# A graph network whose destination one-hots come from TensorE instead of a DRAM broadcast

## The chip, the cores and the metric

The kernel runs on one core of a Trainium2 chip. The metric is the device time of one execution in microseconds (us): the median of 3 runs of the kernel before.

## The reference

There are 6250 nodes with 128 features, and 106,250 directed edges, sorted by destination, self loops among them. Two layers, each with a residual:

```
h = relu(layernorm(x))
m    = leaky_relu(h[src] @ Wl + bl + h[dst] @ Wr + br + ew1 * We)     # layer 1: GATv2
a    = softmax of (m @ att) over the edges of a destination
x    = x + batchnorm(gelu(h + sum over edges(a * (h[src] @ Wl + bl)) + bias))
h = relu(layernorm(x))
em   = relu(layernorm([h[src], h[dst]] @ msg_w + msg_b) * g + beta) * ew   # layer 2
mean = sum over edges(em) / number of edges of the destination
x    = x + gate * relu(layernorm([h, mean] @ upd_w + upd_b)...) + (1 - gate) * h
```

What an edge takes from its source is a row of a node table that lies in DRAM and is gathered by index. What it takes from its destination is spread from a window of the other table by a matmul with a one-hot matrix, as the edges are sorted by destination.

## The kernel before

**Sizes.** Nodes are 49 tiles of 128 (NT). Edges are padded to 832 × 128 and handled in 104 supersteps (NS) of 8 × 128 = 1024 edges (ST, SE). Within a superstep the destinations lie in a window of at most 126 nodes (WIN) above its first.

**Tables.** In lines 233 to 259 the node tiles go in groups of 7 (TG): bn_stats on VectorE, normalization and relu on ScalarE (L248), a transpose on TensorE (L251), a copy of hT by VectorE and ScalarE in turn (L253), a matmul to 257 columns (L255), the add of the bias (L256) for the source table xl and a ScalarE copy (L257) for the destination table xr. SyncE stores both to DRAM (xl_d L258, xr_d L259). After the first group the source indices are cast and transposed (L262). Then a flag read from the data picks general() or fast(); here it is fast().

**Preparation in fast()** (L744 to 843). The destinations relative to the window's first node, dl_b (bf16, one row per superstep), are stored to DRAM as dl_d, and also transposed into columns dl_c. Edge weights and segment marks become columns as well.

**First edge stage** (L886 to 1085). Its instructions keep the order in which they are written (manual_schedule). Superstep s: load(s + 2) has SyncE fetch the window W of the table (L854), row s of dl_d broadcast to 128 partitions (dlb, 256 KB, L856) and the edge weights as a row; GpSimd gathers the sources in 8 indirect DMAs (L196, 10 buffers gl); TensorE spreads the destinations of s + 1 (L867, 16 matmul records); VectorE adds (L1033); ScalarE does relu; a step of the segment maxima; the one-hot oh by destination of u = s − 7 is made (L1040), ScalarE scales the gathered rows (glw, L1049); VectorE multiplies by att and reduces (L1051, L1053); one_hot_t(s + 2) (L863) compares dlb with the partition's number, which gives the one-hot that spreads; TensorE aggregates u (L1063). Generators (nodes, turn) do the node work of finished windows in steps between supersteps.

**Middle** (to L1175): batch normalization, and the tables a_d and b_d of the second layer.

**Second edge stage** (L1177 to 1333), u = s − 1, also in written order: load, 8 gathers into 6 buffers gl1, spread1(s + 1) on TensorE (L867), VectorE's add y (L1298), ScalarE's 8 squares with their sums (L1303) and root (L1304), the store of an aggregate, the one-hot oh of u (L1309), 8 passes with mg_r (L1314), the add of mb_r (L1316), ScalarE's relu (L1317) and glw (L1320), one_hot_t(s + 2) (L863), the reciprocal (L1324), and the aggregation of u (L1329, 16 matmul records). nodes1 gives node work in steps at the end of a superstep (TensorE L1228 to 1269 through the PSUM tiles nt and nz, VectorE L1211 to 1273).

The lines that set the order in stage 2, before:

```
spread1(s + 1)                                   # PE
V.tensor_tensor(y, pss.pop(s), gl, ALU.add)      # DVE L1298
V.tensor_tensor(oh, ...)                         # DVE L1309
for j in range(ST): V.scalar_tensor_tensor(yu, ..., mg_r, ...)   # L1314
V.tensor_tensor(yu, yu, over_tiles(mb_r, ST), ALU.add)           # L1316
S.activation(yu, yu, AF.Relu)                    # ACT L1317
...
one_hot_t(*wins[s + 2])                          # DVE L863
...
T.matmul(aggs[u], oh[:, j, :], glw[:, j, :], ...)  # PE L1329
```

Of the kernel before, what the change touches and what calls it, by code (L numbers as in the profile page):

```python
# [9 lines left out]
F32 = mybir.dt.float32  # L10
# [6 lines left out]
P = 128  # L17
# [18 lines left out]
BT = K // NBT  # L36
WIN = 126
PACE = 60
SLACK = 96
# [9 lines left out]
def kernel(  # L49
# [36 lines left out]
    def flat(v, ap, offset=0):  # L86
        return bass.AP(tensor=v.tensor, offset=v.offset + offset, ap=ap)
# [5 lines left out]
    V.memset(x_sb[:, NT - 1, :], 0.0)  # L93
    for g in range(NG):
        n = TG if g < NG - 1 else TG - 1
        nc.sync.dma_start(
            x_sb[:, g * TG : g * TG + n, :],
            x[g * TG * P : (g * TG + n) * P, :].rearrange("(t p) f -> p t f", p=P),
        )
# [74 lines left out]
    def over_tiles(row, n):  # L174
        return row[:, None, :].to_broadcast([P, n, D])
# [24 lines left out]
    def node_rows(table, g, n=TG):  # L200
        return table[g * TG * P : (g * TG + n) * P].rearrange("(t p) ... -> p t ...", p=P)
# [16 lines left out]
    with tc.tile_pool(name="pre", bufs=2) as pp, tc.tile_pool(name="pre1", bufs=1) as p1, tc.tile_pool(  # L218
# [5 lines left out]
        wt = p1.tile([P, D], F32, name="wt")  # L224
        w0c = p1.tile([P, 2 * D + 1], F32, name="w0c")
        b0c = p1.tile([P, WL], F32, name="b0c")
        V.tensor_copy(w0c[:, WL:], w0[:, D:])
        for o, i in ((w0c, w0), (b0c, b0)):
# [3 lines left out]
            V.tensor_scalar(o[:, D : D + 1], o[:, D : D + 1], 0.2, None, op0=ALU.mult)  # L232
        for g in range(NG):
            mv = pp.tile([P, TG, 2], F32, name="mv")
            for j in range(TG):
                st = pp.tile([P, 6], F32, name="st")
                V.bn_stats(st, x_sb[:, g * TG + j, :])
                V.bn_aggr(mv[:, j, :], st)
            rstd = pp.tile([P, 2, TG], F32, name="rstd0")
            S.activation(rstd[:, 0, :], mv[:, :, 1], AF.Sqrt, bias=eps)  # L240
            V.reciprocal(rstd[:, 0, :], rstd[:, 0, :])
            V.scalar_tensor_tensor(rstd[:, 1, :], mv[:, :, 0], -1.0, rstd[:, 0, :],
                                   op0=ALU.mult, op1=ALU.mult)
            tl = pp.tile([P, TG, WL], F32, name="tl")
            tr = pp.tile([P, TG, D], F32, name="tr")
            for j in range(TG):
                h = pp.tile([P, D], F32, name="h")
                S.activation(h, x_sb[:, g * TG + j, :], AF.Relu, bias=rstd[:, 1, j : j + 1],  # L248
                             scale=rstd[:, 0, j : j + 1])
                tp = ps_p.tile([P, P], F32, name="tp")  # L250
                T.transpose(tp, h, ident)  # L251
                hT = h_sb[:, g * TG + j, :]
                (S.copy if j % 2 else V.tensor_copy)(hT, tp)  # L253
                mm = ps_p.tile([P, 2 * D + 1], F32, name="mm")
                T.matmul(mm, hT, w0c, start=True, stop=True)  # L255
                V.tensor_tensor(tl[:, j, :], mm[:, :WL], b0c, ALU.add)  # L256
                S.copy(tr[:, j, :], mm[:, WL:])  # L257
            nc.sync.dma_start(node_rows(xl_d, g), tl)  # L258
            nc.sync.dma_start(node_rows(xr_d, g), tr)  # L259
            if g == 0:  # L260
                sr = p1.tile([NS, SE], F32, name="sr")
                V.tensor_copy(sr, src_r)  # L262
                columns(ps_k, src_c, sr, "ctp")
# [477 lines left out]
    def fast():  # L741
# [6 lines left out]
        b_d = dram.tile([NP + P, D], F32, name="b_d")  # L748
        dl_d = dram.tile([NS, SE], BF16, name="dl_d")
        res0_d = [dram.tile([NP + P, W0], F32, name=f"res0_{i}") for i in range(2)]  # L750
# [3 lines left out]

        dl_c = fs.tile([P, NS, ST], F32, name="dl_c")
        ew_c = fs.tile([P, NS, ST], F32, name="ew_c")
# [3 lines left out]
        nc.sync.dma_start(base_row, flat(dst, [[1, 1], [SE, NS]]))  # L760

        def base_of(s):
            return nc.values_load(base_row[0:1, s : s + 1], engines=[mybir.EngineType.SP],
                                  min_val=0, max_val=NP - 1)

# [19 lines left out]
        with tc.tile_pool(name="col1", bufs=1) as p1, tc.tile_pool(name="rows", bufs=2) as rp, tc.tile_pool(  # L785
            name="ps_p", bufs=2, space=PSUM
        ) as ps_p:
# [4 lines left out]
            dl_b = p1.tile([NS, SE], BF16, name="dl_b")  # L792
            V.tensor_copy(dl_b, fr)
            nc.sync.dma_start(dl_d, dl_b)

# [49 lines left out]
        def zero(tables, n, i):  # L845

            for r in tables:
                nc.sync.dma_start(r.rearrange("(p k) f -> p (k f)", p=P)[:, i * 5 * n : (i + 1) * 5 * n],
                                  zt[:, : 5 * n])

        def load(pool, table, s, weights):

            w, oht = Ws[s % 3], ohts[s % 3]
            nc.sync.dma_start(w[:WIN], table[ds(base_of(s), WIN), :])  # L854
            dlb = pool.tile([P, SE], BF16, name="dlb")
            nc.sync.dma_start(dlb, flat(dl_d, [[0, P], [1, SE]], s * SE))  # L856
            if weights:
                nc.sync.dma_start(oht[WIN : WIN + 1, :], flat(edge_weight1, [[SE, 1], [1, SE]], s * SE))
            return w, dlb, oht

        def one_hot_t(w, dlb, oht):

            V.tensor_scalar(oht[:WIN, :], dlb[:WIN, :], iota_p[:WIN, :], None, op0=ALU.is_equal)  # L863

# [4 lines left out]
        def store(agg, tables, s):  # L869
            nc.sync.dma_start(tables[s % 2][ds(base_of(s), WIN), :], agg[:WIN, :])  # L870

        def fetch(fin, tables, t0, n):
# [13 lines left out]
        with tc.tile_pool(name="e0", bufs=2) as ep, tc.tile_pool(  # L886
# [3 lines left out]
        ) as ps_m, tc.tile_pool(name="ps_1", bufs=1, space=PSUM) as ps_1, tc.manual_schedule():  # L890
            iota_ps = ps_1.tile([P, P], F32, name="iota_ps")
            S.copy(iota_ps, iota_f)
            LAG = SB + 3
# [107 lines left out]
            def spread(s):  # L1001
                w, _, oht = wins.pop(s)
                pss[s] = ps_m.tile([P, ST, D], F32, name="m_ps")
                expand(pss[s], oht, w)
# [12 lines left out]
            for s in range(2):  # L1017
                one_hot_t(*wins[s])
            spread(0)
            for s in range(NS + LAG + 1):  # L1020
# [16 lines left out]
                if 0 <= u < NS:  # L1037
                    b, q = divmod(u, SB)
                    oh = ep.tile([P, ST, P], F32, name="oh")
                    V.tensor_tensor(oh, over_tiles(iota_ps, ST), over_features(dl_c[:, u, :], ST),  # L1040
                                    ALU.is_equal)
                    glw = ep.tile([P, ST, W0], F32, name="glw")
                    V.tensor_copy(glw[:, :, D:], exm[b][:, q])  # L1043
                if u >= 1:
                    flush(u - 1)
# [132 lines left out]
        with tc.tile_pool(name="e1g", bufs=6) as gp, tc.tile_pool(name="e1", bufs=2) as ep, tc.tile_pool(  # L1178
# [3 lines left out]
        ) as ps_m, tc.tile_pool(name="ps_11", bufs=1, space=PSUM) as ps_1, tc.manual_schedule():  # L1182
            iota_ps = ps_1.tile([P, P], F32, name="iota_ps1")
            S.copy(iota_ps, iota_f)
            glws = [e1.tile([P, ST, WL], F32, name=f"glw1_{i}") for i in range(3)]
# [6 lines left out]
            def spread1(s):  # L1192
                w, _, oht = wins.pop(s)
                pss[s] = ps_m.tile([P, ST, D], F32, name="y_ps")
                expand(pss[s], oht, w)
# [87 lines left out]
            for s in range(2):  # L1283
                one_hot_t(*wins[s])
            spread1(0)
            for s in range(NS + 2):
# [20 lines left out]
                if 0 <= u < NS:  # L1307
                    oh = ep.tile([P, ST, P], F32, name="oh1")
                    V.tensor_tensor(oh, over_tiles(iota_ps, ST), over_features(dl_c[:, u, :], ST),  # L1309
                                    ALU.is_equal)  # L1310
                    yu = ys.pop(u)
                    ru = rss.pop(u)
                    for j in range(ST):
                        V.scalar_tensor_tensor(yu[:, j, :], yu[:, j, :], ru[:, j : j + 1], mg_r,  # L1314
                                               op0=ALU.mult, op1=ALU.mult)
                    V.tensor_tensor(yu, yu, over_tiles(mb_r, ST), ALU.add)  # L1316
                    S.activation(yu, yu, AF.Relu)  # L1317
                    glw = glws[u % 3]
                    for j in range(ST):
                        S.activation(glw[:, j, :D], yu[:, j, :], AF.Copy, scale=ew_c[:, u, j : j + 1])  # L1320
                if s + 2 < NS:
                    one_hot_t(*wins[s + 2])
                if s < NS:
# [61 lines left out]
```

## Time and profile before

| what | value |
|---|---|
| median of 3 runs | 2407.45 us (2405.77 to 2409.37) |
| the profiled execution | 2414.23 us, its span 2412.4 us |
| granted TensorE clock, mean | 0.764 |
| busy: PE, DVE, ACT, POOL | 57%, 68%, 53%, 70% of the span |
| first edge stage, gathers | 71.6 to 1145.7 us |
| middle | 1145.7 to 1256.8 us |
| second edge stage, gathers | 1256.8 to 2355.2 us |
| DMA moved | 242.90 MB, mean 101 GB/s |

PE is TensorE, DVE VectorE, ACT ScalarE, POOL GpSimd, SP SyncE. A group row gives line, engine, operation, output<-input, count, then busy us, mean ns, and the engine's idle time before it with what ended it. A source row gives the minimum, median and maximum in ns, then the first and the last start in us. A row of waits gives the total in us, the times and the longest. A timeline row begins with start and duration in us. L12 is line 12 of the kernel.

### The profile page before, as it was taken

The numbers are of one execution on the slowest core, as the hardware profiler recorded it, in microseconds if no ns is written. First come the engines' busy times: TensorE is split into PE (matmuls) and PEld (weight loads), VectorE is DVE, ScalarE is ACT, GpSimd is POOL, SyncE is SP. The second block draws the span as 40 slices with busy tenths as digits, with TensorE's granted clock in tenths as the row PEclk, the third lists the DMA queues.
The fourth block names the chain that finished last, engine by engine and source line by source line (L and its number), as shares of the span: only waits on it lengthen the run. The fifth ranks groups of instructions, "written<-read, shape, count | busy, mean of one in ns | idle before, by whom it ended". The sixth has DMA issues, their size and how long they took to land.

```text
span 2412.4 us, 30614 instructions
## 1 busy us (share of the span) xinstructions
PE 1375.8 (57%) x7692; PEld 1270.8 (53%) x7692; DVE 1637.3 (68%) x3597; ACT 1276.6 (53%) x4267; POOL 1699.7 (70%) x1703
## 2 busy tenths in 40 slices
PE   6446555556566556565484555555655655555553
PEld 3345555555555455565464555555555654555553
DVE  6666677677677667767445567677767768768765
ACT  5223343334344334344456676676676677667663
POOL 1677777777777777777057777777777777777770
PEclk9667887787878777777687677778777777777876
DMA  6743455443443433443142333343333333333331
GB/s 166 211 114 92 111 151 137 98 100 92 101 100 92 98 96 92 100 100 80 32 132 79 90 94 99 85 107 97 83 107 97 85 108 103 83 101 102 85 96 30
DMA packets 217496, 242.90 MB, mean 101 GB/s; under 512 B 41373, under 2 KB 158077, under 8 KB 217309
## 3 DMA queue, kind: packets, MB, share of 16 engines
q0 software_dynamic: 53792, 110.57, 19.7%
q1 hardware_dynamic: 160657, 130.00, 18.5%
q8 instruction: 64, 1.05, 0.2%
q14 instruction: 123, 1.01, 0.1%
q10 hardware_dynamic: 2860, 0.27, 0.1%
HBM read 197.43 MB, written 43.25 MB: 100 GB/s over the span
## 4 chain that ended last, share of the span: by engine, by line
POOL 44%; issue 18%; DMA 14%; DVE 13%; PE 7%; ACT 3%; SPq 0%; DVEq 0%; another core or an unknown queue 0%; ACTq 0%; POOLq 0%
POOL gl L196 44%; DMA gl<-xl_d,src_c 7%; DMA gl<-a_d,src_c 5%; DVE y L1314 2%; DVE m_ps L1033 2%; PE agg_ps L1063 2%; DVE y L1298 1%; DVE oh L1309 1%; PE agg_ps L1329 1%; DVE y L1316 1%; PE mm L255 1%; PE mm L1156 1%; ACT sq L1303 1%; DVE oh L1040 1%; DVE oht L863 1%
## 5 line engine op out<-in xcount | busy, mean ns | idle before, releaser
L196 POOL DMA_INDIRECT gl<-xl_d,src_c x832 | 820.9, 987 | 308.8 <-issue 229.8
L196 POOL DMA_INDIRECT gl<-a_d,src_c x832 | 845.2, 1016 | 260.7 <-issue 234.3
L1329 PE MATMUL agg_ps<-glw,oh 128*128 128x129 f32 x1664 | 363.9, 403 | 485.7 <-ACT glw L1320 439.7
L1329 PEld LDWEIGHTS agg_ps<-glw,oh 128*128 128x128 f32 x1664 | 336.3, 298 | 505.8 <-ACT glw L1320 505.8
L1063 PE MATMUL agg_ps<-glw,oh 128*128 128x130 f32 x1664 | 345.0, 389 | 386.3 <-DVE glw L1043 206.8
L1063 PEld LDWEIGHTS agg_ps<-glw,oh 128*128 128x128 f32 x1664 | 320.7, 288 | 404.1 <-ACT glw L1049 404.1
L1034 ACT ACTIVATE m_ps<-m_ps 128x1024 f32<-128x1024 f32 x104 | 104.8, 1008 | 573.6 <-DVE m_ps L1033 429.3
L1303 ACT ACTIVATE sq<-y 128x128 f32<-128x128 f32 x832 | 257.1, 309 | 275.8 <-DVE y L1298 252.4
L1033 DVE TENSOR_TENSOR m_ps<-m_ps,gl 128x1024 f32<-128x1024 f32 x104 | 128.1, 1232 | 299.9 <-DMA gl<-xl_d,src_c 273.7
L867 PE MATMUL m_ps<-W,oht 128*128 128x128 f32 x1664 | 259.8, 320 | 36.2 <-DVE oht L863 22.8
L867 PEld LDWEIGHTS m_ps<-W,oht 128*128 128x128 f32 x1664 | 243.8, 233 | 45.2 <-issue 22.3
L1320 ACT ACTIVATE glw<-y,ew_c 128x128 f32<-128x128 f32 x832 | 254.4, 389 | 3.4
L1049 ACT ACTIVATE glw<-gl,exm 128x128 f32<-128x128 f32 x832 | 254.3, 394 | 0.0
L1298 DVE TENSOR_TENSOR y<-y_ps,gl 128x1024 f32<-128x1024 f32 x104 | 126.8, 1220 | 187.8 <-DMA gl<-a_d,src_c 146.7
L867 PE MATMUL y_ps<-W,oht 128*128 128x128 f32 x1664 | 230.4, 298 | 13.2 <-DVE oht L863 9.0
L867 PEld LDWEIGHTS y_ps<-W,oht 128*128 128x128 f32 x1664 | 226.7, 218 | 13.8 <-issue 13.8
L1314 DVE SCALAR_TENSOR_TENSOR y<-y,rs,mg_r 128x128 f32<-128x128 f32 x832 | 227.3, 344 | 0.0
L863 DVE TENSOR_SCALAR oht<-dlb,iota_p 126x1024 f32<-126x1024 bf16 x208 | 159.3, 766 | 15.1 <-DMA dlb<-dl_d 15.0
L1303 ACT ACTIVATION_READ_ACCUMULATOR sq<-y 128x1 f32 x832 | 155.0, 186 | 0.0
L1051 DVE TENSOR_TENSOR m_ps<-m_ps,att 128x1024 f32<-128x1024 f32 x104 | 131.3, 1263 | 4.8 <-ACT m_ps L1034 4.6
L1317 ACT ACTIVATE y<-y 128x1024 f32<-128x1024 f32 x104 | 109.9, 1057 | 41.1 <-DVE y L1316 41.0
L1316 DVE TENSOR_TENSOR y<-y,mb_r 128x1024 f32<-128x1024 f32 x104 | 127.7, 1228 | 3.6
(251 smaller groups left out, 1610.7 us busy)
## 6 DMA issues: line engine op xcount, KB each, us to landing
dlb<-dl_d SPq DMA_DIRECT2D x208, 256.0 KB
gl<-xl_d,src_c POOLq DMA_INDIRECT x832
gl<-a_d,src_c POOLq DMA_INDIRECT x832
res<-agg SPq DMA_DIRECT2D x104, 64.0 KB
res<-agg SPq DMA_DIRECT2D x104, 63.5 KB
W<-xr_d SPq DMA_DIRECT2D x104, 63.0 KB
W<-b_d SPq DMA_DIRECT2D x104, 63.0 KB
res<-zt SPq DMA_DIRECT2D x20, 325.0 KB
```

The lines of the kernel that those rows point to most:

```text
L196: GP.indirect_dma_start(out=dest, out_offset=None, in_=table, in_offset=bass.IndirectOffsetOnAxis(ap=idx, axis=0))
L863: V.tensor_scalar(oht[:WIN, :], dlb[:WIN, :], iota_p[:WIN, :], None, op0=ALU.is_equal)
L867: T.matmul(ps[:, j, :], oht[:, j * P : (j + 1) * P], w, start=True, stop=True)
L1033: V.tensor_tensor(ps, ps, gl[:, :, :D], ALU.add)
L1049: S.activation(glw[:, j, :D], glu[:, j, :D], AF.Copy, scale=exm[b][:, q, j, 1:2])
L1063: T.matmul(aggs[u], oh[:, j, :], glw[:, j, :], start=(j == 0), stop=(j == ST - 1))
L1298: V.tensor_tensor(y, pss.pop(s), gl, ALU.add)
L1303: S.activation(sq, y[:, j, :], AF.Square, accum_out=rs[:, j : j + 1])
L1314: V.scalar_tensor_tensor(yu[:, j, :], yu[:, j, :], ru[:, j : j + 1], mg_r, op0=ALU.mult, op1=ALU.mult)
L1316: V.tensor_tensor(yu, yu, over_tiles(mb_r, ST), ALU.add)
L1320: S.activation(glw[:, j, :D], yu[:, j, :], AF.Copy, scale=ew_c[:, u, j : j + 1])
L1329: T.matmul(aggs[u], oh[:, j, :], glw[:, j, :], start=(j == 0), stop=(j == ST - 1))
```

## The change

- The tables before the branch are made in groups of 6 tiles (PG), three tiles to a PSUM tile (PB), with one copy and one add for three; they hold the source table xl alone. The source indices are cast after the fourth group.
- The destination table xr is made in fast(), 13 chunks of up to 4 tiles (TN).
- dl_b stays in SBUF, and the DRAM copy and the broadcast loads are gone. one_hot_t handles one half of a superstep: TensorE spreads row s of dl_b to all partitions by a matmul with a column of a bf16 identity, into PSUM, and VectorE compares from there. The PSUM tile is one that the node work uses too (tag "mx" in stage 1, "nt" in stage 2). The first half stands ahead of the stage's passes on u, the second where the whole stood.
- The window's first node is loaded into a register once per superstep and kept for the store.
- The column numbers, mg_r and mb_r are copied to PSUM at the start of a stage and read from there.

```diff
@@ tables before the branch @@
-        for g in range(NG):
+        for t0 in range(0, NT, PG):
+            n = min(PG, NT - t0)
...
+            for q in range(0, n, PB):
+                k = min(PB, n - q)
+                tp = ps_p.tile([P, PB, P], F32, name="tp")
+                for j in range(q, q + k):
...
+                    T.transpose(tp[:, j - q, :], h, ident)
+                S.copy(h_sb[:, t0 + q : t0 + q + k, :], tp[:, :k, :])
+                mm = ps_p.tile([P, PB, WL], F32, name="mm")
+                for j in range(k):
+                    T.matmul(mm[:, j, :], h_sb[:, t0 + q + j, :], w0c, start=True, stop=True)
+                V.tensor_tensor(tl[:, q : q + k, :], mm[:, :k, :],
+                                b0c[:, None, :].to_broadcast([P, k, WL]), ALU.add)
...
-                (S.copy if j % 2 else V.tensor_copy)(hT, tp)
-                mm = ps_p.tile([P, 2 * D + 1], F32, name="mm")
-                T.matmul(mm, hT, w0c, start=True, stop=True)
-                V.tensor_tensor(tl[:, j, :], mm[:, :WL], b0c, ALU.add)
-                S.copy(tr[:, j, :], mm[:, WL:])
-            nc.sync.dma_start(node_rows(xl_d, g), tl)
-            nc.sync.dma_start(node_rows(xr_d, g), tr)
-            if g == 0:
+            nc.sync.dma_start(xl_d[t0 * P : (t0 + n) * P].rearrange("(t p) f -> p t f", p=P), tl[:, :n, :])
+            if t0 == 3 * PG:
@@ fast(), preparation @@
+            if s not in bases:
+                bases[s] = nc.values_load(base_row[0:1, s : s + 1], engines=[mybir.EngineType.SP],
+                                          min_val=0, max_val=NP - 1)
+            return bases[s]
...
-            nc.sync.dma_start(dl_d, dl_b)
+            for t0 in range(0, NT, TN):
+                n = min(TN, NT - t0)
+                rp_ = ps_x.tile([P, TN, D], F32, name="xr_ps")
+                for j in range(n):
+                    T.matmul(rp_[:, j, :], h_sb[:, t0 + j, :], w0[:, D:], start=True, stop=True)
+                tr = xp.tile([P, TN, D], F32, name="tr")
+                S.copy(tr[:, :n, :], rp_[:, :n, :])
+                nc.sync.dma_start(xr_d[t0 * P : (t0 + n) * P].rearrange("(t p) f -> p t f", p=P), tr[:, :n, :])
@@ fast(), helpers @@
+        def constants(pool, *rows_):
+            n = 1 + len(rows_)
+            t = pool.tile([P, n * P], F32, name="cst")
+            for k, r in enumerate((iota_f,) + rows_):
+                S.copy(t[:, k * P : (k + 1) * P], r)
+            return [t[:, k * P : (k + 1) * P] for k in range(n)]
...
-            dlb = pool.tile([P, SE], BF16, name="dlb")
-            nc.sync.dma_start(dlb, flat(dl_d, [[0, P], [1, SE]], s * SE))
...
-        def one_hot_t(w, dlb, oht):
-            V.tensor_scalar(oht[:WIN, :], dlb[:WIN, :], iota_p[:WIN, :], None, op0=ALU.is_equal)
+        def one_hot_t(pool, tag, s, k, w, oht):
+            es = slice(k * CH, (k + 1) * CH)
+            dlp = pool.tile([P, CH], F32, name="dlp", tag=tag)
+            T.matmul(dlp, ident_b[:NS, s : s + 1].to_broadcast([NS, P]), dl_b[:, es], start=True, stop=True)
+            V.tensor_scalar(oht[:WIN, es], dlp[:WIN, :], iota_p[:WIN, :], None, op0=ALU.is_equal)
@@ first edge stage, after oh and the copy into glw @@
+                if s + 2 < NS:
+                    one_hot_t(ps_1, "mx", s + 2, 0, *wins[s + 2])
                 if u >= 1:
                     flush(u - 1)
...
                 if s + 2 < NS:
-                    one_hot_t(*wins[s + 2])
+                    one_hot_t(ps_1, "mx", s + 2, 1, *wins[s + 2])
@@ second edge stage, after oh @@
+                if s + 2 < NS:
+                    one_hot_t(ps_1, "nt", s + 2, 0, *wins[s + 2])
+                if 0 <= u < NS:
                     yu = ys.pop(u)
                     ru = rss.pop(u)
                     for j in range(ST):
-                        V.scalar_tensor_tensor(yu[:, j, :], yu[:, j, :], ru[:, j : j + 1], mg_r,
+                        V.scalar_tensor_tensor(yu[:, j, :], yu[:, j, :], ru[:, j : j + 1], mg_ps,
                                                op0=ALU.mult, op1=ALU.mult)
-                    V.tensor_tensor(yu, yu, over_tiles(mb_r, ST), ALU.add)
+                    V.tensor_tensor(yu, yu, over_tiles(mb_ps, ST), ALU.add)
...
                 if s + 2 < NS:
-                    one_hot_t(*wins[s + 2])
+                    one_hot_t(ps_1, "nt", s + 2, 1, *wins[s + 2])
```

More of the change, by code (lines that the diff above doesn't have):

```diff
@@ L37 @@
 WIN = 126
+PG = 6
+PB = 3
 PACE = 60
@@ L93 @@
     V.memset(x_sb[:, NT - 1, :], 0.0)
-    for g in range(NG):
-        n = TG if g < NG - 1 else TG - 1
+    for g in range(NT // PG):
         nc.sync.dma_start(
-            x_sb[:, g * TG : g * TG + n, :],
-            x[g * TG * P : (g * TG + n) * P, :].rearrange("(t p) f -> p t f", p=P),
+            x_sb[:, g * PG : (g + 1) * PG, :],
+            x[g * PG * P : (g + 1) * PG * P, :].rearrange("(t p) f -> p t f", p=P),
         )
@@ L224 @@
         wt = p1.tile([P, D], F32, name="wt")
-        w0c = p1.tile([P, 2 * D + 1], F32, name="w0c")
+        w0c = p1.tile([P, WL], F32, name="w0c")
         b0c = p1.tile([P, WL], F32, name="b0c")
-        V.tensor_copy(w0c[:, WL:], w0[:, D:])
         for o, i in ((w0c, w0), (b0c, b0)):
@@ L232 @@
             V.tensor_scalar(o[:, D : D + 1], o[:, D : D + 1], 0.2, None, op0=ALU.mult)
-        for g in range(NG):
-            mv = pp.tile([P, TG, 2], F32, name="mv")
-            for j in range(TG):
+        for t0 in range(0, NT, PG):
+            n = min(PG, NT - t0)
+            mv = pp.tile([P, PG, 2], F32, name="mv")
+            for j in range(n):
                 st = pp.tile([P, 6], F32, name="st")
-                V.bn_stats(st, x_sb[:, g * TG + j, :])
+                V.bn_stats(st, x_sb[:, t0 + j, :])
@@ L238 @@
                 V.bn_aggr(mv[:, j, :], st)
[L239 to L242, printed above, removed]
+            rstd = pp.tile([P, 2, PG], F32, name="rstd0")
+            S.activation(rstd[:, 0, :n], mv[:, :n, 1], AF.Sqrt, bias=eps)
+            V.reciprocal(rstd[:, 0, :n], rstd[:, 0, :n])
@@ L243 @@
+            V.scalar_tensor_tensor(rstd[:, 1, :n], mv[:, :n, 0], -1.0, rstd[:, 0, :n],
                                    op0=ALU.mult, op1=ALU.mult)
[L244 to L252, printed above, removed]
-                (S.copy if j % 2 else V.tensor_copy)(hT, tp)
-                mm = ps_p.tile([P, 2 * D + 1], F32, name="mm")
-                T.matmul(mm, hT, w0c, start=True, stop=True)
-                V.tensor_tensor(tl[:, j, :], mm[:, :WL], b0c, ALU.add)
-                S.copy(tr[:, j, :], mm[:, WL:])
@@ L258 @@
-            nc.sync.dma_start(node_rows(xl_d, g), tl)
-            nc.sync.dma_start(node_rows(xr_d, g), tr)
-            if g == 0:
+            tl = pp.tile([P, PG, WL], F32, name="tl")
+            for q in range(0, n, PB):
+                k = min(PB, n - q)
+                tp = ps_p.tile([P, PB, P], F32, name="tp")
+                for j in range(q, q + k):
+                    h = pp.tile([P, D], F32, name="h")
+                    S.activation(h, x_sb[:, t0 + j, :], AF.Relu, bias=rstd[:, 1, j : j + 1],
+                                 scale=rstd[:, 0, j : j + 1])
+                    T.transpose(tp[:, j - q, :], h, ident)
[5 more added lines that the diff above has]
+                                b0c[:, None, :].to_broadcast([P, k, WL]), ALU.add)
@@ L748, in fast @@
         b_d = dram.tile([NP + P, D], F32, name="b_d")
-        dl_d = dram.tile([NS, SE], BF16, name="dl_d")
         res0_d = [dram.tile([NP + P, W0], F32, name=f"res0_{i}") for i in range(2)]
@@ L755, in fast @@
         dl_c = fs.tile([P, NS, ST], F32, name="dl_c")
+        dl_b = fs.tile([NS, SE], BF16, name="dl_b")
+        ident_b = fs.tile([P, P], BF16, name="ident_b")
+        V.tensor_copy(ident_b, ident)
         ew_c = fs.tile([P, NS, ST], F32, name="ew_c")
@@ L760, in fast @@
         nc.sync.dma_start(base_row, flat(dst, [[1, 1], [SE, NS]]))
+        bases = {}
         def base_of(s):
-            return nc.values_load(base_row[0:1, s : s + 1], engines=[mybir.EngineType.SP],
-                                  min_val=0, max_val=NP - 1)
+            if s not in bases:
+                bases[s] = nc.values_load(base_row[0:1, s : s + 1], engines=[mybir.EngineType.SP],
+                                          min_val=0, max_val=NP - 1)
+            return bases[s]
         kbrk = fs.tile([NBT, BT, P + 1], BF16, name="kbrk")
@@ L785, in fast @@
         with tc.tile_pool(name="col1", bufs=1) as p1, tc.tile_pool(name="rows", bufs=2) as rp, tc.tile_pool(
-            name="ps_p", bufs=2, space=PSUM
-        ) as ps_p:
+            name="xr", bufs=2
+        ) as xp, tc.tile_pool(name="ps_p", bufs=2, space=PSUM) as ps_p, tc.tile_pool(
+            name="ps_x", bufs=2, space=PSUM
+        ) as ps_x:
             base_f = p1.tile([NS, 1], F32, name="base_f")
@@ L791, in fast @@
             V.tensor_scalar(fr, dst_r, base_f, None, op0=ALU.subtract)
-            dl_b = p1.tile([NS, SE], BF16, name="dl_b")
             V.tensor_copy(dl_b, fr)
-            nc.sync.dma_start(dl_d, dl_b)
+            for t0 in range(0, NT, TN):
+                n = min(TN, NT - t0)
+                rp_ = ps_x.tile([P, TN, D], F32, name="xr_ps")
+                for j in range(n):
+                    T.matmul(rp_[:, j, :], h_sb[:, t0 + j, :], w0[:, D:], start=True, stop=True)
+                tr = xp.tile([P, TN, D], F32, name="tr")
+                S.copy(tr[:, :n, :], rp_[:, :n, :])
+                nc.sync.dma_start(xr_d[t0 * P : (t0 + n) * P].rearrange("(t p) f -> p t f", p=P), tr[:, :n, :])
             for w in Ws:
@@ L854, in load @@
             nc.sync.dma_start(w[:WIN], table[ds(base_of(s), WIN), :])
-            dlb = pool.tile([P, SE], BF16, name="dlb")
-            nc.sync.dma_start(dlb, flat(dl_d, [[0, P], [1, SE]], s * SE))
             if weights:
                 nc.sync.dma_start(oht[WIN : WIN + 1, :], flat(edge_weight1, [[SE, 1], [1, SE]], s * SE))
-            return w, dlb, oht
-        def one_hot_t(w, dlb, oht):
-            V.tensor_scalar(oht[:WIN, :], dlb[:WIN, :], iota_p[:WIN, :], None, op0=ALU.is_equal)
+            return w, oht
+        def one_hot_t(pool, tag, s, k, w, oht):
[3 more added lines that the diff above has]
+            V.tensor_scalar(oht[:WIN, es], dlp[:WIN, :], iota_p[:WIN, :], None, op0=ALU.is_equal)
         def expand(ps, oht, w):
@@ L870, in store @@
             nc.sync.dma_start(tables[s % 2][ds(base_of(s), WIN), :], agg[:WIN, :])
+            del bases[s]
         def fetch(fin, tables, t0, n):
@@ L890, in fast @@
         ) as ps_m, tc.tile_pool(name="ps_1", bufs=1, space=PSUM) as ps_1, tc.manual_schedule():
-            iota_ps = ps_1.tile([P, P], F32, name="iota_ps")
-            S.copy(iota_ps, iota_f)
+            (iota_ps,) = constants(ps_1)
             LAG = SB + 3
@@ L1001, in spread @@
             def spread(s):
-                w, _, oht = wins.pop(s)
+                w, oht = wins.pop(s)
                 pss[s] = ps_m.tile([P, ST, D], F32, name="m_ps")
@@ L1017, in fast @@
             for s in range(2):
-                one_hot_t(*wins[s])
+                for k in range(2):
+                    one_hot_t(ps_1, "mx", s, k, *wins[s])
             spread(0)
@@ L1182, in fast @@
         ) as ps_m, tc.tile_pool(name="ps_11", bufs=1, space=PSUM) as ps_1, tc.manual_schedule():
-            iota_ps = ps_1.tile([P, P], F32, name="iota_ps1")
-            S.copy(iota_ps, iota_f)
+            iota_ps, mg_ps, mb_ps = constants(ps_1, mg_r, mb_r)
             glws = [e1.tile([P, ST, WL], F32, name=f"glw1_{i}") for i in range(3)]
@@ L1192, in spread1 @@
             def spread1(s):
-                w, _, oht = wins.pop(s)
+                w, oht = wins.pop(s)
                 pss[s] = ps_m.tile([P, ST, D], F32, name="y_ps")
@@ L1283, in fast @@
             for s in range(2):
-                one_hot_t(*wins[s])
+                for k in range(2):
+                    one_hot_t(ps_1, "nt", s, k, *wins[s])
             spread1(0)
```

## The prediction

> **What bounds the kernel now.** I read the page's chain first, then the cost rows of the gathers with their source view, then the waits, then one superstep in the timeline.
>
> ```profile
> POOL 44%; issue 18%; DMA 14%; DVE 13%; PE 7%; ACT 3%; SPq 0%; DVEq 0%; another core or an unknown queue 0%; ACTq 0%; POOLq 0%
> L196 POOL DMA_INDIRECT gl<-xl_d,src_c x832: 940/944/1701, 71.6 to 1144.8; - x167
> L196 POOL DMA_INDIRECT gl<-a_d,src_c x832: 940/945/1954, 1256.8 to 2354.3; - x167
> ```
>
> POOL issues gathers almost without a hole. Each stage has 832 of them, 0.944 us at the median with 0.30 us of "issue" between: 832 × 1.249 = 1039 us, or 9.99 us per superstep of eight. The stages take 1073 and 1098 us (10.3 and 10.55 per superstep). The excess is in long gathers (maxima 1701 and 1954 ns): the busy sums are 820.9 and 845.2 us against 832 × 0.944 = 785.4, so 35.5 and 59.8 us. In the timeline the long ones lie beside one_hot_t (L863, SBUF to SBUF) and L1314/L1316 (two SBUF inputs), as at 1507.38 below.
>
> That is a bound with little beneath it: PE runs its instructions in order, and in stage 2 it stands idle where it need not.
>
> ```profile
> PE agg_ps L1329 <- ACT glw L1320: 439.7, 97, 11.8
> DVE z L1240 <- PE nz L1237: 82.6, 13, 7.8
> ```
> ```profile
> 1504.35 2.18 DVE L1314 SCALAR_TENSOR_TENSOR y<-y,rs,mg_r 128x128 f32<-128x128 f32 x8
> 1506.56 1.22 DVE L1316 TENSOR_TENSOR y<-y,mb_r 128x1024 f32<-128x1024 f32 x1
> 1507.38 1.22 POOL L196 DMA_INDIRECT gl<-a_d,src_c  x1 [0.30 <-issue]
> 1507.70 0.75 DVE L863 TENSOR_SCALAR oht<-dlb,iota_p 126x1024 f32<-126x1024 bf16 x1
> 1507.82 1.06 ACT L1317 ACTIVATE y<-y 128x1024 f32<-128x1024 f32 x1 [0.56 <-DVE y L1316]
> 1508.91 2.45 ACT L1320 ACTIVATE glw<-y,ew_c 128x128 f32<-128x128 f32 x8
> 1509.36 3.81 PE L1329 MATMUL agg_ps<-glw,oh 128*128 128x129 f32 x16 [7.27 <-ACT glw L1320]
> 1512.96 2.62 PE L867 MATMUL y_ps<-W,oht 128*128 128x128 f32 x16
> ```
>
> The spread (L867) has had its one-hot since 1508.45 at the latest, yet starts only when the aggregation before it, waiting 7.27 us for glw, is done. From the first L1314 to the end of that spread it takes 1515.58 − 1504.35 = 11.23 us; call it Q. Measured so wherever aggregation and spread follow each other directly, Q is 9.4 to 11.8, mean 10.6; where PE had idled 4 to 6 us before the aggregation it is 10.3 to 11.8, about 11.0 (aggregation mostly 3.5 to 3.8, spread 1.95 to 3.2). Now this costs nothing: the y that needs the spread is added a superstep later, so the way round may take two supersteps.
>
> **The change, part by part.** Sums go against the profiled execution: 2414.2 us, span 2412.4, 1.8 around it. The median of the runs shown is 2407.45, 6.8 lower.
>
> *First table.* Before, ACT sets the pace: per tile relu 0.495, its share of the copies of hT 21 × 0.263 / 49 = 0.11, the xr copy 0.262: 0.87, and the last 41 tiles take 35.6 us (29.8 to 65.4). After: relu 0.495 and a third of a 128x384 copy, scaled from the 128x512 row (586 ns) to 0.44, so 0.15: 0.645. 41 × 0.225 = 9 us. The last store carries 64 KB, not 451 + 448 KB (landing 5.2 us now): 2 to 3 more. The src cast still waits for src_r at 29.2, but stands behind the third and not the first group. I take −12; −6 if the flag's read on SP becomes last, −17 if the 6 us stall at 23.7 goes too.
>
> *Second table in fast().* 13 chunks: up to 4 matmuls of 128 columns (0.3 each), one ACT copy (0.59), one 256 KB store (landing in 2.3 to 3 us for a_d). PE 15 us, ACT 8 us, the stores in a row on SP some 30 us. W of superstep 0 needs them, so the first spread and add come late. POOL fills ten gl buffers meanwhile, 100 us of gathers; before, the add followed its gathers by 17 us at the start, now by 25 to 30. With DVE's demand of some 7.9 us per superstep against POOL's 10 it catches up. Cost nothing; uncovered it would be 10 to 15 us.
>
> *Loads.* 208 loads of 256 KB and the dl_d round trip go, and half the values_loads. DMA is 35% to 41% busy in the stages and only 15 us of DVE's waits name dlb: nothing, either way a few us.
>
> *One-hot from PSUM, constants in PSUM.* No SBUF-to-SBUF pass and no two-SBUF-input pass is left beside stage 2's gathers, and L863's go from stage 1. If POOL stays the bound, all but 5 to 10 us of the excess comes back: −27 in stage 1 (0 to −36), −50 in stage 2. PSUM operands cost DVE nothing that shows: L1298 with one (1220) stands beside L1316 (1228), L1240 (343) beside L1314 (344).
>
> *The broadcast matmul and where its compare stands.* New per superstep: two bf16 matmuls of 128x512 and two compares. The matmul: from below L867's 128x128 (298 ns mean), from above L1126's f32 128x512 (665); I take 0.45, near the middle. The compare: from below half of L863 (0.38), from above L984 (0.744); I take L1273's 0.69, a 128x512 pass with a PSUM operand.
>
> A rule of the Trainium skill speaks here against the change: "VectorE: DVE Perf Modes", section "Why PSUM operands drop a tier", says an fp32 PSUM operand holds DVE at its base rate, so the two halves would not share out L863's time. No row of before shows it for this pass; by half of L863 the period below would be 0.31 shorter and the sum 2559.
>
> In stage 1 the maxima, the one-hot oh, the copy of glw and ACT's glw do not wait for the first compare. PE's way round is matmul 0.45, compare 0.69, matmul 0.45 (same PSUM buffer), aggregation 3.3 to 3.8, spread 2.5, with the transposes 8 to 8.6 us: below 9.99. POOL stays the bound.
>
> In stage 2 the first compare stands ahead of L1314 on DVE. Its matmul, for s+2, stands on PE behind spread(s+1), which stands behind the aggregation of u = s−2. That waits for glw, this for relu, L1316 and L1314 of the same u, and those for the compare of the superstep before. The ring now closes in one superstep: Q 11.0 + matmul 0.45 + compare 0.69 = 12.1 us, above POOL's 9.99 and the 10.55 now. Queued behind the waiting compare are L1314, L1316, the second compare, the next y; PE idles meanwhile.
>
> Bounds of the period: with Q 9.4 and the cheap ends 0.30 and 0.38, 10.1; with Q 11.8, 0.67 and 0.74, 13.2. The nodes' generator puts PE work between aggregation and spread: per group 4 transposes 0.75, the nz step 2.0 plus 1.2 of DVE, the last step 1.1 plus 1.9: 7 us, for 10 groups 70. From the first gather to the last L1314 in the ring: 24.5 (start, as now) + 100 × 12.1 + 70 = 1304.5, against 2339.7 − 1256.8 = 1082.9 now: +222. The ends give +22 and +332. The tail after it (72.7 us) and the middle (1145.7 to 1256.8) keep their rows.
>
> The ring stands only if a ready matmul cannot pass a waiting one; the 439.7 us above show that it does not. In the ring PE pauses for compare, L1314, L1316, relu and the first glw, 0.69 + 3.45 + 1.1 + 0.4 = 5.6 us, broken only by the second broadcast; rows with such a pause gave the 11.0.
>
> The skill's "TensorE: Matmul & The Clock Gate", section "HAM oscillation — how this bites in real kernels", says that pauses over about 3.4 us throttle PE's clock again each time. The rows agree in kind (aggregation 2.54 after pauses under 2.5 us, mostly 3.5 to 3.8 after 4 to 6); taken strictly, every ring would run at the long end, Q 11.8, and the sum would be 2670.
>
> **Sum.** 2412.4 − 12 − 27 + 222 = 2595.4; + 1.8 − 6.8 = 2590 us.
>
> **Rivals.** *POOL remains the bound (faster).* One mechanism: the ring takes less than 9.99 us. For it: the shortest Q seen (9.4) with the cheapest ends gives 10.1, and the records show a granted clock that varies (0.76 mean in this stretch). Against: Q is that short only where PE idled under 2.5 us before the aggregation, and the ring itself makes 5 to 6 us of idleness. Time: 2412.4 − 12 − 27 − 50 − 5 = 2318. It decides where the period is under 10.5. Chance 0.12.
>
> *A milder ring.* The second broadcast in PE's pause keeps aggregation and spread short: Q 9.6 to 10.1, period 10.7 to 11.2: 100 × 1.2 less, 2470. Chance 0.2, within the range.
>
> *Stage 1 also slows.* If its aggregation and spread wait as in stage 2, the period there is 10.5 to 11 and not 10.0: +52 to +104, 2640 to 2690. Against: nothing there stands between the compare and ACT's glw. Chance 0.12.
>
> *The contention is elsewhere than I read it*, and the long gathers stay: stage 1 gives nothing, 2617; within the range, 0.1.
>
> **How the numbers follow.** The ring at 11.6 to 12.6 has 0.44, and the range of the ring's cases together is 2450 to 2660; outside lie the first rival (0.12) and the far end of the third. What a measurement here can tell from no change is 0.2%, 5 us. Slower by more 0.86, faster 0.12, within 0.02.
>
> **What would show it.** Right: in stage 2 a superstep of about 12 us, POOL's gaps over 0.3 us and waiting for gl buffers, DVE waiting at the first compare for PE's broadcast, long gathers gone or without effect; in stage 1 a superstep of 10.0 and gathers with a mean near 0.95; the first gather near 60 us. Wrong: POOL solid in stage 2 with a period of 10.0; the compare not waiting; stage 1's add waiting for PE beyond its first supersteps.

## The result, and the profile after

The changed kernel takes 2577.38 us in the median of 4 runs (2574.63 to 2583.33), the kernel before 2408.41 beside it: 1.0706 times as long, with a 95% interval of 1.0683 to 1.0728. Forecast: 2590, range 2450 to 2660, slower with 0.86.

The page's chain of the changed kernel, by engine, then the source view of the gathers (line 197 now) with the releasers of their idle time:

```profile
PE 29%; DVE 28%; POOL 18%; issue 10%; DMA 7%; ACT 7%; SPq 0%; DVEq 0%; ACTq 0%; POOLq 0%
```
```profile
L197 POOL DMA_INDIRECT gl<-xl_d,src_c x832: 940/944/2509, 62.6 to 1107.1; - x167
L197 POOL DMA_INDIRECT gl<-a_d,src_c x832: 938/944/1393, 1225.5 to 2460.3; - x167
...
  issue: 467.5, 1534
  DVE y L1326: 205.6, 34
```

POOL, 44% of the chain before, is 18% of it. Its first stage is still solid and now without long gathers: 1045.5 us from the first start to the last end, where 832 at 1.249 are 1039. In the second the gathers are as short (they sum to 785.7 us against 845.2), yet the stage takes 1235.7 us, since POOL stands 205.6 us until the add (L1326) has freed a gl buffer.

The waits of the changed kernel (total us, times, longest):

```profile
PE agg_ps L1360 <- ACT glw L1351: 462.7, 104, 6.5
DVE oht L888 <- PE dlp L887: 358.7, 123, 5.8
ACT y L1348 <- DVE y L1347: 321.5, 102, 5.3
PE dlp L887 <- DVE oht L888: 309.0, 207, 6.6
...
POOL gl L197 <- DVE y L1326: 205.6, 34, 9.7
```

Every one of the 104 aggregations waits for glw, and the compare for the broadcast: the first and second lines are two links of a ring, the third is a third. One turn of it in the timeline of the changed kernel:

```profile
1600.38 3.81 PE L1360 MATMUL agg_ps<-glw,oh 128*128 128x129 f32 x16 [4.46 <-ACT glw L1351]
...
1603.98 2.83 PE L892 MATMUL y_ps<-W,oht 128*128 128x128 f32 x16
...
1606.64 0.38 PE L887 MATMUL dlp<-dl_b,ident_b 104*128 104x512 bf16 x1
1607.07 0.75 DVE L888 TENSOR_SCALAR oht<-dlp,iota_p 126x512 f32<-126x512 f32 x1 [5.28 <-PE dlp L887]
...
1607.73 2.15 DVE L1345 SCALAR_TENSOR_TENSOR y<-y,rs,cst 128x128 f32<-128x128 f32 x8
...
1609.91 1.22 DVE L1347 TENSOR_TENSOR y<-y,cst 128x1024 f32<-128x1024 f32 x1
...
1611.16 1.06 ACT L1348 ACTIVATE y<-y 128x1024 f32<-128x1024 f32 x1 [4.98 <-DVE y L1347]
...
1612.25 2.45 ACT L1351 ACTIVATE glw<-y,ew_c 128x128 f32<-128x128 f32 x8
1612.71 3.65 PE L1360 MATMUL agg_ps<-glw,oh 128*128 128x129 f32 x16 [4.46 <-ACT glw L1351]
```

Read from top to bottom, each line starts within 0.2 us of the end of the one above it (the aggregation after the first of eight glw), and the last line is the first of the next turn. VectorE has nothing to do for 5.28 us and TensorE for 4.46, in turn. 1612.71 − 1600.38 = 12.33 us; POOL could feed one in 9.99.

### The profile page after: what moved, and what is told of

Same layout as the page of the kernel before. It is cut to its first block, busy times and chain, and to the rows that moved or that the text cites. A ratio compares the mean times of both kernels' runs of the same rounds, so it can differ in the third digit from the quotient of the medians.

```text
span 2574.6 us, 30564 instructions
## 1 busy us (share of the span) xinstructions
PE 1496.1 (58%) x8206; PEld 1313.1 (51%) x8206; DVE 1750.5 (68%) x3749; ACT 1277.8 (50%) x4231; POOL 1611.3 (63%) x1703
## 3 DMA queue, kind: packets, MB, share of 16 engines
q1 hardware_dynamic: 130732, 75.25, 10.4%
## 4 chain that ended last, share of the span: by engine, by line
PE 29%; DVE 28%; POOL 18%; issue 10%; DMA 7%; ACT 7%; SPq 0%; DVEq 0%; ACTq 0%; POOLq 0%
POOL gl L197 18%; PE agg_ps L1360 15%; DVE y L1345 8%; PE y_ps L892 7%; DVE y L1347 5%; DMA gl<-xl_d,src_c 5%; ACT y L1348 4%; DVE oht L888 4%; DVE m_ps L1059 2%; ACT glw L1351 2%; PE m_ps L892 1%; PE agg_ps L1091 1%; DVE y L1326 1%; DVE oh L1337 1%; PE dlp L887 1%
## 5 line engine op out<-in xcount | busy, mean ns | idle before, releaser
L197 POOL DMA_INDIRECT gl<-a_d,src_c x832 | 785.7, 944 | 457.2 <-issue 231.9
L197 POOL DMA_INDIRECT gl<-xl_d,src_c x832 | 792.2, 952 | 299.1 <-issue 235.6
L1360 PE MATMUL agg_ps<-glw,oh 128*128 128x129 f32 x1664 | 389.1, 427 | 462.7 <-ACT glw L1351 462.7
L888 DVE TENSOR_SCALAR oht<-dlp,iota_p 126x512 f32<-126x512 f32 x416 | 309.5, 744 | 358.7 <-PE dlp L887 358.7
L887 PE MATMUL dlp<-dl_b,ident_b 104*128 104x512 bf16 x416 | 169.4, 407 | 426.2 <-DVE oht L888 309.0
L1091 PE MATMUL agg_ps<-glw,oh 128*128 128x130 f32 x1664 | 304.9, 359 | 20.0 <-ACT glw L1077 15.3
L892 PEld LDWEIGHTS y_ps<-W,oht 128*128 128x128 f32 x1664 | 243.6, 232 | 8.4 <-issue 6.7
L892 PE MATMUL y_ps<-W,oht 128*128 128x128 f32 x1664 | 245.8, 311 | 0.0
L1345 DVE SCALAR_TENSOR_TENSOR y<-y,rs,cst 128x128 f32<-128x128 f32 x832 | 223.2, 341 | 0.0
L1326 DVE TENSOR_TENSOR y<-y_ps,gl 128x1024 f32<-128x1024 f32 x104 | 124.7, 1199 | 21.7 <-DMA gl<-a_d,src_c 21.0
L1081 DVE TENSOR_REDUCE lr<-m_ps 128x8 f32<-128x1024 f32 x104 | 127.4, 1225 | 3.6
```

The lines of the kernel that those rows point to most:

```text
L197: GP.indirect_dma_start(out=dest, out_offset=None, in_=table, in_offset=bass.IndirectOffsetOnAxis(ap=idx, axis=0))
L887: T.matmul(dlp, ident_b[:NS, s : s + 1].to_broadcast([NS, P]), dl_b[:, es], start=True, stop=True)
L888: V.tensor_scalar(oht[:WIN, es], dlp[:WIN, :], iota_p[:WIN, :], None, op0=ALU.is_equal)
L892: T.matmul(ps[:, j, :], oht[:, j * P : (j + 1) * P], w, start=True, stop=True)
L1091: T.matmul(aggs[u], oh[:, j, :], glw[:, j, :], start=(j == 0), stop=(j == ST - 1))
L1360: T.matmul(aggs[u], oh[:, j, :], glw[:, j, :], start=(j == 0), stop=(j == ST - 1))
```

## The experiments

Two theories. The ring: with the first compare ahead of L1314, the chain above closes within one superstep. The work: two compares of 0.744 us (the source view of L888 has 727/744/752 ns) for one of 0.747, and two broadcasts of 0.38, are simply too much. Line numbers are those of each kernel. Ratios are to the kernel before, measured beside it on the same chip; where there is no interval it is one run.

### The late compare

```diff
-                if s + 2 < NS:
-                    one_hot_t(ps_1, "nt", s + 2, 0, *wins[s + 2])
                 if 0 <= u < NS:
                     yu = ys.pop(u)
...
                 if s + 2 < NS:
-                    one_hot_t(ps_1, "nt", s + 2, 1, *wins[s + 2])
+                    for k in range(2):
+                        one_hot_t(ps_1, "nt", s + 2, k, *wins[s + 2])
```

> The changed kernel with one edit: in the second edge stage the first compare stands where the second does, behind L1316, relu and glw. All the work is the same. The ring theory (broadcast behind spread behind aggregation behind glw behind the compare): the ring is open, POOL is the bound again, superstep 9.99 us, stage 2's gathers take 1040 to 1050 us (1235.7 in the changed kernel), the tail behind the last gather shrinks from 113 to about 57 us, 2330 us in all (2320 to 2345). The work theory (two 0.74 us passes from PSUM and two broadcasts more per superstep are what costs): no change, 2570 to 2585.

The first four kernels fell on a chip where the kernel before takes 2988.16 us (2981.73 to 3007.09), and there the late compare took 3180.3, a ratio of 1.0618 (1.057 to 1.0666). Three rows of the late compare's waits there show why nothing follows for the ring:

```profile
DVE oht L888 <- remote: 684.3, 75, 39.4
...
PEld agg_ps L1359 <- issue: 271.6, 21, 35.7
PEld L887 <- issue: 252.4, 62, 12.5
```

In its first stage (300 to 1100 us) TensorE, VectorE and ScalarE stand still together 25 times, for 4 to 12 us, and of the wait that ends last the profile says "remote" or "issue", which names no releaser on this core. GpSimd does not stop with them, against what the next expectation says of all engines: it goes on gathering until its buffers are full.

```profile
698.57 0.95 POOL L197 DMA_INDIRECT gl<-xl_d,src_c  x1 [0.30 <-issue]
...
706.07 0.95 POOL L197 DMA_INDIRECT gl<-xl_d,src_c  x1 [0.30 <-issue]
...
707.67 0.75 DVE L888 TENSOR_SCALAR oht<-dlp,iota_p 126x512 f32<-126x512 f32 x1 [11.77 <-remote]
```

POOL bounds neither stage there, and the changed kernel itself was not run on that chip. The other three on that chip: constants in SBUF 3171.41 (1.0601; 1.0548 to 1.0655), broadcast first 3215.22 in one run, the kernel before with its compare early 2986.35 in one run. What the pauses are stays open. All four were run again on other chips, where the kernel before takes 2412 to 2413 us; the expectations below are those of the second time.

> The late compare once more, as the first run of it fell on a chip where the kernel before takes 2988 us and all engines pause together for 6 to 13 us every 30 us or so. Where the kernel before takes about 2408 us, the ring theory expects 2330 us (2320 to 2345), stage 2's gathers within 1040 to 1050 us; the work theory 2570 to 2585. Where the pauses come again, both expect what was seen: 1.06 times the kernel before.

Measured: 2325.56 us, a ratio of 0.9645 (0.9619 to 0.9671), so 0.90 of the changed kernel's time by moving one broadcast with its compare; the order of TensorE's instructions is the same in both traces. It is the fastest version of this study, ahead of both kernels. Its source view of the gathers:

```profile
L197 POOL DMA_INDIRECT gl<-xl_d,src_c x832: 940/944/1619, 62.2 to 1104.6; - x167
L197 POOL DMA_INDIRECT gl<-a_d,src_c x832: 940/944/1461, 1224.3 to 2265.2; - x167
...
  issue: 472.4, 1550
```

From 1224.3 to the last end at 2266.2 are 1041.9 us, three above the floor; the 205.6 us of waiting for the add are gone, and behind the last gather there are 58.2 us and not 113.4. The work is all still there (416 broadcasts and 416 compares in both): the work theory has fallen.

### The broadcast ahead of the spread

```diff
+                if s + 2 < NS:
+                    dlp0 = ps_1.tile([P, CH], F32, name="dlp", tag="nt")
+                    T.matmul(dlp0, ident_b[:NS, s + 2 : s + 3].to_broadcast([NS, P]), dl_b[:, :CH], start=True, stop=True)
                 if s + 1 < NS:
                     spread1(s + 1)
...
-                    one_hot_t(ps_1, "nt", s + 2, 0, *wins[s + 2])
+                    V.tensor_scalar(wins[s + 2][1][:WIN, :CH], dlp0[:WIN, :], iota_p[:WIN, :], None, op0=ALU.is_equal)
```

> The first broadcast ahead of the spread on TensorE, the compare still early. Ring theory: the ring loses the spread (2.4 us in the mean), 12.4 - 2.4 = 10.0 us, about 10.3 with the node work: 2335 to 2385 us. Work theory: 2570 to 2585.

Measured: 2415.09 us in one run, 162 less than the changed kernel and 30 above the expected range. In its trace the first twelve whole periods, ahead of the node work, are 9.4 to 11.4 us, 10.1 in the mean; in the changed kernel 11.9. But 10.1 is POOL's pace here, and the late compare has 10.1 too: in most of these turns the add waits for its gather and the compare for nothing. What is left of the ring shows later, where gathers lie ready and the compare waits for its broadcast again:

```profile
1268.68 1.22 DVE L1329 TENSOR_TENSOR y<-y_ps,gl 128x1024 f32<-128x1024 f32 x1 [2.94 <-DMA gl<-a_d,src_c]
...
1550.46 0.75 DVE L1343 TENSOR_SCALAR oht<-dlp,iota_p 126x512 f32<-126x512 f32 x1 [2.40 <-PE dlp L1324]
```

The plain ones of those turns mostly take 9.3 to 9.7 us, so the ring has lost some 2.4 us, as expected. With the node work the mean of the first 100 periods is 10.91 and not the 10.3 that I had: its slowest supersteps still take 13.9 to 14.6 us, a node step that waits for TensorE being in the ring all the same.

### An older u

```diff
-            due = rounds_of(1)
+            due = rounds_of(2)
...
-            for s in range(NS + 2):
-                u = s - 1
+            for s in range(NS + 3):
+                u = s - 2
```

The pool of y has four buffers here, three before.

> The changed kernel with u = s - 2 in the second stage (was s - 1), and a fourth y buffer: L1314 and what follows handle a superstep that is one older. Ring theory: the ring holds one compare, one aggregation and one spread whatever the age of u, so the period stays 12.4 us and the end comes one superstep later: 2580 to 2600 us. Slack theory (the changed kernel only lacks lead between the add and L1314): POOL is the bound again, 2330 to 2360 us.

Measured: 2590.89 us in one run, 13.5 above the changed kernel. The first twelve periods are 11.9 us as there. More lead does not help, as the ring does not hold the age of u.

### The kernel before, with its compare early

```diff
+                if s + 2 < NS:
+                    one_hot_t(*wins[s + 2])
+                if 0 <= u < NS:
                     yu = ys.pop(u)
...
-                if s + 2 < NS:
-                    one_hot_t(*wins[s + 2])
```

> The kernel before with its SBUF one_hot_t ahead of L1314. Ring theory: no TensorE in its way, 2400 to 2420 us. Position theory: 80 us more, 2488.

Measured: 2439.71 us in one run, 27 above the kernel before beside it: neither. POOL remains solid (its longest gap in the stage is 0.32 us), so there is no ring, and 80 us of position are not there either. The 27 are in the gathers, whose group row is

```profile
L196 POOL DMA_INDIRECT gl<-a_d,src_c x832 | 875.1, 1052 | 260.6 <-issue 237.1
```

875.1 − 845.2 = 29.9 us more than before: contention, which the next two pursue.

### Which passes hold up the gathers

The late compare with constants in SBUF, then the kernel before with constants in PSUM:

```diff
-                        V.scalar_tensor_tensor(yu[:, j, :], yu[:, j, :], ru[:, j : j + 1], mg_ps,
+                        V.scalar_tensor_tensor(yu[:, j, :], yu[:, j, :], ru[:, j : j + 1], mg_r,
...
-                    V.tensor_tensor(yu, yu, over_tiles(mb_ps, ST), ALU.add)
+                    V.tensor_tensor(yu, yu, over_tiles(mb_r, ST), ALU.add)
```

> The late compare with the constants mg_r and mb_r in SBUF instead of PSUM. Contention with two-SBUF-input passes: 24 us (15 to 35) more than the late compare alone (2325.6), 2350 us, and gathers of stage 2 with maxima near 2 us again. All of the excess from L863: within 5 us of it.

```diff
-            iota_ps = ps_1.tile([P, P], F32, name="iota_ps1")
-            S.copy(iota_ps, iota_f)
+            cst = ps_1.tile([P, 3 * P], F32, name="cst")
+            for k, r in enumerate((iota_f, mg_r, mb_r)):
+                S.copy(cst[:, k * P : (k + 1) * P], r)
...
-                        V.scalar_tensor_tensor(yu[:, j, :], yu[:, j, :], ru[:, j : j + 1], mg_r,
+                        V.scalar_tensor_tensor(yu[:, j, :], yu[:, j, :], ru[:, j : j + 1], mg_ps,
...
-                    V.tensor_tensor(yu, yu, over_tiles(mb_r, ST), ALU.add)
+                    V.tensor_tensor(yu, yu, over_tiles(mb_ps, ST), ALU.add)
```

> The kernel before with one edit: L1314 and L1316 read their constants from PSUM; L863 stays from SBUF in its old place. Stage 2's gathers summed 845.2 us before and 845.1 with the SBUF constants alone, against 788.6 with neither; stage 1 with L863 alone 820.9. If each kind of pass holds up gathers by itself, L863 alone is left: 816 to 825 us in stage 2 and 2380 to 2390 us in all. If L863 next to relu costs stage 2 nothing: 790 us and 2355.

Measured: 2379.22 us (ratio 0.9846; 0.9798 to 0.9893) and 2370.6 us (0.9825; 0.98 to 0.9849). The first is 54 above the late compare alone (48 by the two ratios, as the chips differ), twice what I expected. The second gains 40 and lies between its two expectations. The group rows of the stage 2 gathers, in this order:

```profile
L197 POOL DMA_INDIRECT gl<-a_d,src_c x832 | 845.1, 1016 | 260.5 <-issue 237.1
```
```profile
L196 POOL DMA_INDIRECT gl<-a_d,src_c x832 | 804.6, 967 | 260.7 <-issue 239.2
```

| passes beside stage 2's gathers | busy sum, us | above 785.4 |
|---|---|---|
| none (late compare) | 788.6 | 3 |
| L863 alone, behind the add of mb | 804.6 | 19 |
| the constants' passes alone | 845.1 | 60 |
| both, L863 right behind the add of mb (before) | 845.2 | 60 |
| both, L863 ahead of L1314 | 875.1 | 90 |

Two profiles with the same passes in the same places differ by up to 5 us (845.2 here, 850.1 in the last experiment below), and each row is one profile. To that accuracy the constants' passes cost all of it by themselves. L863 stands right behind the add, where the same gather is already held, and adds nothing there; put elsewhere it meets gathers of its own and adds 30. Summed over the long gathers (over 0.98 us) of each trace, this can be seen: those under the add carry 47 us of excess before and 49 with the constants' passes alone, those under L1314 only 8 to 10, and where L863 stands early the gathers under it carry 20 of their own. How a gather is held shows in the timeline of the late compare with constants in SBUF:

```profile
1515.87 1.22 DVE L1345 TENSOR_TENSOR y<-y,mb_r 128x1024 f32<-128x1024 f32 x1
1516.17 1.74 POOL L197 DMA_INDIRECT gl<-a_d,src_c  x1 [0.31 <-issue]
...
1518.21 0.94 POOL L197 DMA_INDIRECT gl<-a_d,src_c  x1 [0.30 <-issue]
```

It begins under the add, and ends 0.82 us after the add has ended (1517.91 − 1517.09), nearly a whole gather later.

### TensorE kept busy in the ring's pause

```diff
-                    one_hot_t(ps_1, "nt", s + 2, 1, *wins[s + 2])
+                    dlp = ps_1.tile([P, CH], F32, name="dlp", tag="nt")
+                    for _ in range(9):
+                        T.matmul(dlp, ident_b[:NS, s + 2 : s + 3].to_broadcast([NS, P]), dl_b[:, CH:], start=True, stop=True)
+                    V.tensor_scalar(wins[s + 2][1][:WIN, CH:], dlp[:WIN, :], iota_p[:WIN, :], None, op0=ALU.is_equal)
```

> The changed kernel with one edit: in the second stage the second broadcast is issued nine times into the same tile, so TensorE is busy for 2 to 3.4 us of the pause of about 5 us in the ring; the compares stay. If the pause is what makes aggregation and spread long (3.65 to 3.81 and 1.95 to 2.85 us, against 2.54 and 1.95 after short pauses), the plain period falls from 11.9 to 10.4 to 10.9 us: 2430 to 2490 us. If the lengths have another reason, nothing falls: 2575 to 2620.

Measured: 2499.55 us in one run, 78 less than the changed kernel, 10 outside the expected range. In the timeline:

```profile
1361.54 2.15 DVE L1345 SCALAR_TENSOR_TENSOR y<-y,rs,cst 128x128 f32<-128x128 f32 x8
1361.67 2.10 PE L1355 MATMUL dlp<-dl_b,ident_b 104*128 104x512 bf16 x9 [0.84 <-DVE oht L888]
...
1366.51 2.54 PE L1363 MATMUL agg_ps<-glw,oh 128*128 128x129 f32 x16 [2.74 <-ACT glw L1351]
...
1368.88 1.95 PE L892 MATMUL y_ps<-W,oht 128*128 128x128 f32 x16
```

With 2.74 us of pause left the aggregation takes 2.54 us and the spread 1.95, and the plain periods are 10.2 us one after the other, 1.7 shorter than in the changed kernel, and shorter than I expected. From 1255 to 1380 us, ahead of the node work, the granted clock is 1.00, in the changed kernel 0.72. The windows of both kernels from 1300 to 2300 us (PE, PEld, DVE, ACT, POOL busy, then the granted clock), this one first:

```profile
1300.00:2300.00 1000.00, 677.50 (x3789) 531.95 (x3788) 684.47 (x1528) 619.08 (x2326) 673.70 (x713) 0.87 0.28 66
```
```profile
1300.00:2300.00 1000.00, 553.36 (x2950) 500.72 (x2951) 639.60 (x1427) 584.40 (x2191) 631.08 (x669) 0.73 0.26 62
```

More work on TensorE made the kernel faster, and the granted clock rose with it. Whether the shorter pause decides or the larger busy share (82.1 against 71.3 us from 1255 to 1380) is not shown, as the copies change both. Around the node work the periods remain 11.4 to 15.1 us, which is why it is 78 us and not 170.

### The tables alone, in the kernel before

```diff
-        for g in range(NG):
+        for t0 in range(0, NT, PG):
...
-            nc.sync.dma_start(node_rows(xr_d, g), tr)
...
             nc.sync.dma_start(dl_d, dl_b)
+            for t0 in range(0, NT, TN):
...
```

These are the first two parts of the change, with both edge stages and their loads as before.

> The kernel before with the change's tables alone: groups of six tiles before the branch, the destination table in the preparation; both edge stages as before, with the broadcast loads and the SBUF one-hot. The prediction's term: -12 us (-6 to -17), from the first gather; in the changed kernel's profile the first gather comes 9.0 us earlier, in other profiles of its kind 71.5 - (62.2 to 72.2) = -0.7 to 9.3. If the stores of the destination table stay hidden behind the gathers: 2396 to 2405 us. If they hold the first adds up so far that POOL runs out of buffers: 2410 or more.

Measured, in 12 runs: 2412.51 us, a ratio of 0.9986 (0.9972 to 1.0000): 2 to 3 us, the end of the interval at none. The time lies in the second range, but not for its reason: POOL does not run out of buffers (stage 1's gathers take 1068.8 us, 1074.2 before). In its profile the first gather is at 70.29, in the changed kernel's at 62.6. The difference is in the pace of the table stage: the last adds (L258, one for three tiles) follow each other in 2.82 us here, in 1.99 there. The windows of that stretch, this kernel first (columns as above):

```profile
44.00:64.00 20.00, 17.02 (x64) 12.91 (x63) 5.62 (x21) 11.84 (x30) 0.00 (x0) 0.50 0.21 60
```
```profile
44.00:57.00 13.00, 9.30 (x56) 6.54 (x55) 4.88 (x16) 10.39 (x26) 0.00 (x0) 1.00 0.32 92
```

At a granted clock of 0.50 TensorE is busy 0.85 of the time (17.02 / 64 = 266 ns a record against 166) and is the busiest engine; at 1.00 ScalarE is (10.39 of 13 us). The code of the table stage is the same in all kernels with the new tables, and yet their first gathers lie anywhere from 62.2 (late compare) to 72.2 us (older u): the pace is not set by the code.

## Why the prediction was right, step by step

| step | forecast, us | by the two profiles, us |
|---|---|---|
| first gather | −12 (−6 to −17) | 62.6 − 71.6 = −9.0 |
| stage 1's gathers | −27 (0 to −36) | 1045.5 − 1074.2 = −28.7 |
| middle | 0 | 117.4 − 111.1 = +6.3 |
| stage 2, first gather to the last L1314 of the ring | +222 (22 to 332) | 1277.9 − 1082.9 = +195.0 |
| behind it | 0 | 71.2 − 72.7 = −1.5 |
| sum | +183 | +162.1; the spans differ by 162.2 |

**The ring** is shown, not argued: opened by the late compare it is gone, without the spread it is some 2.4 us shorter, kept with an older u it is the same. Its Q, put at 11.0 from the pauses of the kernel before, is 11.0: in the first twelve plain turns it alternates between 10.4 and 11.6, by a spread of 1.95 and one of 2.8 to 3.0. Broadcast and compare were put at 0.45 + 0.69 and measured 0.38 + 0.75, but from the end of the spread to the next L1345 there are only 0.92, as the first broadcast starts before the spread's last records end. So the period is 11.9, not 12.1: 18 of the 27 us by which stage 2 was put too high. The node work adds 1253.6 − 100 × 11.92 = 62 us, not 70; the start is 24.3, not 24.5. The 27 us too many in stage 2 are in part made up by the middle's +6.3, so the total is nearer than its largest term.

**The rivals.** *POOL remains the bound* is the time of the late compare (2325.6 against the 2318 that I gave): it needed another place for one compare, not a shorter Q; with the pause filled the plain turn is 10.2 us, still above 9.99. *A milder ring* is the kernel with the filled pause; the second broadcast alone does not do it. *Stage 1 also slows* and *the contention is elsewhere* fell with stage 1's 1045.5 us.

**The rule on PSUM operands** (the Trainium skill, "VectorE: DVE Perf Modes", section "Why PSUM operands drop a tier") is borne out: a 126x512 compare from PSUM takes 0.744 us, the 126x1024 from SBUF 0.747. Likewise "HAM oscillation — how this bites in real kernels" of "TensorE: Matmul & The Clock Gate", in kind: with pauses of 4.46 us, the second broadcast beside them, the granted clock is 0.72; with pauses of 2.74 us it is 1.00. Taken strictly for every turn it gave too long a time, as every second spread is short (1.95 us).

**What I had wrong.** In the expectation for the constants in SBUF I split the excess: the one-hot pass got stage 1's share and the constants the rest, 24 us. The two do not add; the constants' passes cost 845.1 − 788.6 = 56 by themselves. The prediction's sum does not hold this split, since in stage 2 the ring covers the excess. The term for the first table held for a pace of TensorE that not every run has: 9 us in this profile, 2 to 3 in the median of the tables alone. Two readings of the prediction were off without weight in the sum: the source indices are cast behind the fourth group of tiles, not the third, and the 1073 us of stage 1 reach to the last gather's start, 1074.2 to its end. The middle's +6.3 was in no term; profiles of the kernels with the old stages have 111.1 to 115.4 there, those with the new 113.2 to 118.8, and whether the change has a part in it stays open.

## What to carry to other kernels

When a result passes through an in-order engine, count how many supersteps the way round takes, not only each engine's busy time: a compare placed ahead of the passes that the next aggregation waits for closed a chain of three engines within one superstep, and cost 250 us with no engine busy over 70%. Place the reader of a fresh matmul behind the work that the next matmul in that queue waits for. And take a change apart before judging it: what it did to contention was worth 29 us in stage 1 and some 56 in stage 2, and the place of one compare hid that.

## What the runs showed of the hardware that I had not expected

- Passes that hold up the gathers do not always add: L863 alone 19 us, the constants' passes 60, both in a row 60, both apart 90. The gather shown, begun under such a pass, ended 0.82 us after it. To place contending passes back to back was worth as much here (90 to 60) as to remove L863.
- Eight needless copies of a matmul made a kernel 78 us faster, with the granted clock up from 0.73 to 0.87 (1300 to 2300 us).
- One and the same table stage went at 1.99 us for three tiles in one profile and at 2.82 in another. In one kernel with the long pace the clock's record says 1.00 where the durations are those of 0.50 (the older u, 44 to 64 us: 17.03 us for 64 records, 266 ns each): the two disagree, and I went by the durations.
- On one chip of the several used TensorE, VectorE and ScalarE stood still together again and again, and the kernel before took 2988 us and not 2408: a version has to be compared with its neighbour on the same chip.
